# Two graph-attention layers on one core: attention units visited in pairs, three visits a step in place of six

## The chip, the cores and the metric

The kernel runs on one core of one Trainium2 chip. The metric is the device time of one execution in microseconds. Three runs of the kernel before gave 3366.99, 3367.01 and 3368.44 us; the median is 3367.01 us.

## What is computed

64 graphs of 256 nodes with 512 features go through two layers. Each layer normalises the rows, takes the positive part, runs attention over the graph's edges and adds the result to its input. The reference, cut to what matters:

```python
# layer 0: 4 heads of 64, adjacency as mask
h = jnp.maximum(_layernorm(x, axis=-1), 0.0)
q, k, v = h @ Wq, h @ Wk, h @ Wv                       # split in 4 heads
sim = jnp.einsum('bhid,bhjd->bhij', q, k) * scale
attn = softmax(where(adj, sim, -max))
x = x + einsum('bhij,bhjd->bhid', attn, v) @ Wo + bo
# layer 1: 8 heads of 64, another layernorm with gamma and beta, mask = adj | eye
h = jnp.maximum(_layernorm(x, axis=-1), 0.0)
...
x = x + (probs @ v) @ w_out.T + b_out
```

All is in f32.

## The kernel before

**Step and units.** A step works on two graphs (G = 2), so there are 32 steps. Two heads make a *unit* (`pr`): layer 0 has two units a step and layer 1 four, so six a step and 192 in all. The steps overlap: while step s runs its layer 1, step s+1 finishes layer 0 and step s+2 starts it.

**Products.** The projections (`project_qk` L769, `project_v1` L810) and the output products (`combine` L826) each run a two-by-two block product in seven block products instead of eight. That needs sums of blocks, which GpSimd (POOL) forms (`act_sums0`, `act_sums1`, L409 to L414). The seven results are put together by VectorE (DVE) and ScalarE (ACT) in `evacuate` and `accumulate`. Each product writes one of four PSUM banks, handed round by `mm_tile`. `project_v0` (L796) is plain.

**A unit of attention** goes through these pieces:

- `scores` (L877): eight matmuls on half the array each (64 rows, two at once), into four PSUM tiles `sc`, one for each graph g and head e. A tile is 128x512 f32. The pool of these tiles, `ps_sc`, has four buffers.
- `mask_scores` (L901): DVE adds the mask to one score tile and writes `p` in SBUF; four for a unit.
- `exponentials` (L906): ACT, four for a unit, in place on `p`.
- `key_halves` (L911): POOL adds the two halves over keys into `pd`, two for a unit.
- `weigh` (L920): sixteen matmuls on 32 columns each (four at once) into one tile of the same pool `sc`; ACT copies it to `oT` (L937).
- `key_sums` (L953): four matmuls of `pd` with ones, the softmax's denominators, into an `mm` bank.
- `invert` (L963, L964): DVE takes the reciprocals in two halves, and one more operation keeps the extremes. Eight small DMAs (L978), issued by SyncE (SP), spread the result over partitions into `invb`.
- `normalise` (L983): POOL multiplies `oT` by `invb`.

**A visit** joins the end of one unit with the start of another: weighing, sums and inversion of a unit `prev`, then scores and masks of a unit `cur`, whose exponentials and key halves follow.

**What sets the order.** On PE, DVE, ACT and POOL the order is written out by hand: `at(period, place, fn, ...)` collects events, which are sorted by `period * PERIOD + place` and issued in that order. A whole set of seven products has length 1 on this scale, and a step has 6.2. SP is not on the list. [...]

**Order of a step on PE before**, from place 0.0: a visit, then `project_qk` (s,1,0); at 1.0 a visit, `project_v1`; at 2.0 a visit, `project_qk` (s,1,1); at 3.0 a visit, `transpose_h` of s+2 and `combine` of layer 0 of s+1; at 3.64 a visit, `project_qk` (s+2,0,0); at 4.64 a visit, `project_v0`; at 5.2 `transpose_h` of s+1 and `combine` of layer 1 of s.

Of the kernel before, what the change touches and what calls it, by code (L numbers as in the profile page):

```python
# [315 lines left out]
def fast_path(  # L316
# [136 lines left out]
    def weight_loads():  # L453

        pair = act.tile([P, 2, 4, D], FP, name="wr", tag="oT1")
        blocks = [
            pair[:, 0], pair[:, 1],
            act.tile([P, 4, D], FP, name="wr", tag="v1"), io.tile([P, 4, D], FP, name="wr", tag="xt"),
        ]
        for n, wr in enumerate(blocks):  # L460
            src, r0 = (w_qkv, 4 * n) if n < 3 else (w_out, 0)
            nc.sync.dma_start(wr, src[r0 * P:(r0 + 4) * P].rearrange("(r p) i -> p r i", p=P))
        return blocks

    def weight_block(wr, n, c):
        pw = mm_tile([P, 4 * P])
        for r in range(4):
            nc.tensor.transpose(pw[:, r * P:(r + 1) * P], wr[:, r, c * P:(c + 1) * P], ident)
        for i in range(2):
            blk = A_OF[i, c // HC]  # L470
            dst = wqkv1[:, blk, c % HC, n, :] if n < 3 else wo1[:, blk, c % HC, :]
            copy = nc.vector.tensor_copy if i == 0 and (n or c == 0) else nc.scalar.copy
            copy(dst, pw[:, i * H1:(i + 1) * H1])  # L473
# [16 lines left out]
    def load_x(s):  # L490
        xt = io.tile([P, NT, D], FP, name="xt")
        nc.sync.dma_start(xt, x[s * G:(s + 1) * G].rearrange("g (t p) d -> p (g t) d", p=P))
        S[s]["xt"] = xt
# [259 lines left out]
    def project_qk(s, lyr, a, n):  # L753
# [3 lines left out]
        if n == 1:  # L757
            for i, pr in enumerate((a, a + half)):
                if (s, lyr, a) == (NSTEP - 1, 1, 0):
                    tile_qk = wqk0[:, 2 * i:2 * i + 2].rearrange("p n c k o -> p n (c k o)")  # L760
                else:
                    tile_qk = sm.tile([P, 2, T], FP, name="qk", bufs=2)
                st["qk", lyr, pr] = tile_qk
# [101 lines left out]

    units = [0]

    def scores(s, lyr, pr):
# [17 lines left out]
        elif last and pr == 3:  # L886
            p = [act.tile([P, G, NIC, N], FP, name="p", tag=tag) for tag in ("oT0", "v0")]
        else:
            p = [sm.tile([P, G, NIC, N], FP, name="p", bufs=4) for _ in range(2)]
        if last and pr in (1, 2):  # L890
            pd = (wo0[:, :4, 0, :], wv0)[pr - 1].rearrange("p a b -> p (a b)").rearrange("p (e g n) -> p e g n", e=2, g=G)
        else:
            pd = sm.tile([P, 2, G, N], FP, name="pd", bufs=1)
# [14 lines left out]
    def key_halves(s, lyr, pr, e):  # L908
        p, pd = S[s]["p", lyr, pr]
        eng = nc.vector if (s, lyr) == (NSTEP - 1, 1) and pr in (1, 3) else nc.gpsimd  # L910
        eng.tensor_tensor(pd[:, e], p[e][:, :, 0, :], p[e][:, :, 1, :], ALU.add)  # L911

    def weigh(s, lyr, pr, first):
# [11 lines left out]
        if lyr == 0:  # L925
            if first:
                st["oT0"] = act.tile([P, NB, HP0, N], FP, name="oT0")
        elif first:
            st["oT1"] = act.tile([P, NB, HP1, N], FP, name="oT1")
# [5 lines left out]
    def weigh_out(s, lyr, pr, first):  # L935
        po, dst = weigh(s, lyr, pr, first)
# [3 lines left out]
    def weigh_last(pr):  # L940

        po, dst = weigh(NSTEP - 1, 1, pr, pr == 0)
        nc.vector.tensor_tensor(dst, po, S[NSTEP - 1]["invb", 1, pr], ALU.mult)

    def key_sums(s, lyr, pr):

        st = S[s]
        _, pd = st["p", lyr, pr]
        sums = st["sums", lyr, pr] = mm_tile([P, N])
        for g in range(G):  # L950
            for e in range(2):
                r0 = 32 * (2 * g + e)
                nc.tensor.matmul(  # L953
                    sums[r0:r0 + 32, :], ones, pd[:, e, g, :], start=True, stop=True
                )

    def invert(s, lyr, pr):
        st = S[s]
        sums = st.pop(("sums", lyr, pr))
        last = (s, lyr) == (NSTEP - 1, 1)  # L960
        inv = sm.tile([P, N], FP, name="inv", tag="u" if last and pr == 3 else "inv", bufs=1)
        for i in range(2):
            nc.vector.reciprocal(inv[:, i * P:(i + 1) * P], sums[:, i * P:(i + 1) * P])  # L963
# [5 lines left out]
        if last and pr:  # L969
            invb = act.tile([P, G, N], FP, name="invb", tag=("n0", "ne", "ab")[pr - 1])  # L970
        else:
            invb = sm.tile([P, G, N], FP, name="invb", bufs=1)
        for g in range(G):
            for e in range(2):
                r0 = 32 * (2 * g + e)
                for d0 in range(e * DH, (e + 1) * DH, 32):
                    queue = nc.scalar if d0 % DH and last and pr in (1, 3) else nc.sync
                    queue.dma_start(invb[d0:d0 + 32, g, :], inv[r0:r0 + 32, :])  # L978
# [10 lines left out]
    PERIOD = 6.2  # L989
# [3 lines left out]
    def at(period, place, fn, *args):  # L993
        events.append((period * PERIOD + place, len(events), fn, args))
# [15 lines left out]
    def visit(period, w, prev, cur):  # L1010

        w -= 0.0003
        if 0 <= prev[0] < NSTEP:
            at(period, w, weigh_out, *prev)
            at(period, w, key_sums, *prev[:3])
            at(period, w, invert, *prev[:3])
            at(period, w + (0.63 if prev[1:3] == (1, 1) else 0.55), normalise, *prev[:3])
        if 0 <= cur[0] < NSTEP:
            at(period, w, scores, *cur)
            at(period, w, mask_scores, *cur, 0)  # L1020
            at(period, w + 0.05, exponentials, *cur, 0)
            at(period, w + 1 / 7, mask_scores, *cur, 1)
            at(period, w + 0.22, exponentials, *cur, 1)
            at(period, w + 0.23, key_halves, *cur, 0)
            at(period, w + 0.3, key_halves, *cur, 1)

    AT_C0, AT_Q0, AT_V0, AT_H1, AT_C1 = 3.0, 3.64, 4.64, 5.2, 5.201
    LAST_QK = 3.0
    for s in range(-1, NSTEP - 1):
        p, tail = s, s == NSTEP - 2  # L1030
        if s >= 0:
            visit(p, 0.0, (s + 1, 0, 0, True), (s + 1, 0, 1))
            visit(p, 1.0, (s + 1, 0, 1, False), (s, 1, 0))
        visit(p, 2.0, (s, 1, 0, True), (s, 1, 2))
        visit(p, 3.0, (s, 1, 2, False), (s, 1, 1))
        visit(p, LAST_QK + 4 / 7 if tail else AT_Q0, (s, 1, 1, False), (s, 1, 3))
        if s >= 0:
            visit(p, LAST_QK + 1 if tail else AT_V0, (s, 1, 3, False), (s + 1, 1, 0) if tail else (s + 2, 0, 0))

    none = (NSTEP,)  # L1040
    p = NSTEP - 2
    for w, i, pr in ((1, 5 / 7, 0), (1 + 3 / 7, 5 / 7, 2), (2, 5 / 7, 1), (2 + 3 / 7, 5 / 7, 3)):
        if pr:
            visit(p, LAST_QK + w, none, (NSTEP - 1, 1, pr))
        at(p, LAST_QK + w + i - 0.0005, key_sums, NSTEP - 1, 1, pr)
        at(p, LAST_QK + w + i, invert, NSTEP - 1, 1, pr)
# [4 lines left out]
    visit(-2, AT_V0, (-1, 0, 0, True), (0, 0, 0))  # L1051
    visit(-2, AT_H1, (0, 0, 0, True), (0, 0, 1))
    visit(-2, AT_H1 + 0.67, (0, 0, 1, False), (-1, 0, 0))
    visit(-1, 2.3, (-1, 0, 0, False), (1, 0, 0))
    for s in range(NSTEP):

        p = s - 2
        if s == 1:
            p -= 3.93 / PERIOD
        at(p - 1 if s != 1 else -2, 5.7 if s != 1 else 3.2, load_h, s)  # L1060
        at(p, (2.0, 2.4)[s] if s < 2 else 0.2, adjacency_cast, s)
        for t in range(NT):
# [3 lines left out]
            else:  # L1066
                at(p, 2.3 + 0.1 * t if s != 1 else 2.6 + 0.1 * t, scale_row, s, t)
        for g in range(G):
            at(p, (1.8, 2.7)[s] if s < 2 else 0.58 + 0.14 * g, neighbours, s, g)
        if s < 2:  # L1070
            at(p, (2.9, 2.72)[s], neighbours_rows, s)
            at(p, (AT_Q0 + 0.285, 3.59)[s], neighbours_turn, s)
        else:
            at(p, 0.75, neighbours_out, s)
            at(p, 1.9, neighbours_in, s)
        at(p, (AT_Q0 + 0.1425, 3.583)[s] if s < 2 else 2.2, adjacency_turn, s)
        at(p, (AT_Q0 + 0.3, 3.74)[s] if s < 2 else 2.75, mask0, s)
        at(p, (AT_Q0 + 0.31, 4.43)[s] if s < 2 else 5.7, mask1, s)
        if s == 0:
            at(p, AT_C0, first_transposes)  # L1080
# [3 lines left out]
        at(p, AT_C0 + 0.1, lambda s=s: act_sums0(S[s]["hT"]))  # L1084
        at(p, AT_C0 + (0.35 if s > 1 else 0.101 if s else 0.2), lambda s=s: act_sums1(S[s]["hT"]))
        order = SET if s else (1, 2, 6, 5, 7, 3, 4)
        at_set(p, AT_Q0 if s != 1 else 3.3, order, project_qk, s, 0, 0)
        for t in range(NT):
            at_dense(p, AT_V0 + 0.14 * t + (-0.0005 if s == 0 and t == 0 else 0) if s != 1 else (4.31, 5.02, 5.16, 5.31)[t], 0.14, project_v0, s, t)
        p = s - 1  # L1090
        if s == 0:
            p -= 2.23 / PERIOD
        at(p, 0.0 if s == 0 else 1.0 if s < NSTEP - 1 else 0.7, load_x, s)
        at(p, 1.55 if s == 0 else 1.8 if s < NSTEP - 1 else 1.25, first_bias, s)
        if 0 < s < NSTEP - 1:
            at(p, 1.75, lambda s=s: act_sums0(S[s]["oT0"]))
            at(p, 1.76, lambda s=s: act_sums1(S[s]["oT0"]))
        edge = 0 if s == 0 else 1 if s == NSTEP - 1 else 2
        for i, n in enumerate(SETC0 if 0 < s < NSTEP - 1 else NORM1):
            if edge == 0:  # L1100
                at_dense(p, 2.76 + 0.14 * i, 0.14, combine_rows, s, n)
            elif edge == 1:
                at_dense(p, 1.99905 + 0.00014 * i, 0.00113, combine_rows, s, n)
# [111 lines left out]
```

## Time and profile before

| What | Value |
|---|---|
| median of three runs | 3367.01 us |
| the profiled execution's own time | 3368.43 us |
| its span | 3366.6 us |
| granted TensorE clock | 0.999 |
| score matmuls, L877 with tiles `qk` | 3040 records, 380.3 us busy |
| weighing matmuls, L920 | 6144 records, 370.7 us busy |
| mask adds, L901 | 768, 478.6 us busy, 682 ns each |
| reciprocals, L963 | 384, 339.7 us busy, 926 ns each |
| key halves on POOL, L911 | 378, 472.5 us busy, 1271 ns each |
| inverses spread by DMA, L978 | 1528 issues on SP of 32 KB each, 1.9 us to landing |

One f32 matmul leaves two records. A record's duration is longer than the distance between two starts, since matmuls are pipelined, so lengths on PE are best taken from start to start. In the kernel's order of time a step repeats every 104.07 us from the second to the last but one (the first product of `project_v1` starts at 1045.27 us and again at 1149.34 us).

### The profile page before, as it was taken

To read this page: it belongs to the slowest core of one execution; us is meant where nothing else is said; L and a number is where in the kernel's file an instruction comes from. 1 tells how busy PE (TensorE), PEld (TensorE's weight loads), DVE (VectorE), ACT (ScalarE), POOL (GpSimd) and SP (SyncE) were. 2 spreads that over 40 slices of the span, in tenths; PEclk is the share of its full clock that TensorE was granted. 3 is DMA by queue.
4 is the path that set the end of the run, shared out by engine and by line. 5 is a ranking of instruction groups with operands and counts; after the bars stand their busy time and mean duration, and the time that the engine had idled before them with its cause. 6 is when DMAs were issued, how large, how long until landed. Compare 5 with 4: busy or idle time off the path is not lost.

```text
span 3366.6 us, 60168 instructions
## 1 busy us (share of the span) xinstructions
PE 3349.3 (99%) x22962; PEld 2688.2 (80%) x22962; DVE 1938.0 (58%) x3460; ACT 1230.5 (37%) x2218; POOL 2215.4 (66%) x2112
## 2 busy tenths in 40 slices
PE   8999999999999999999999999999999999999999
PEld 6788887888888888888888788887888878888877
DVE  6655556555565555555555655556555565565656
ACT  4333333333343334433344333443333333334331
POOL 6766775666766667666676566775667766667642
PEclk9999999999999999999999999999999999999999
DMA  3122111221112211112211121111111111211111
GB/s 130 46 59 57 54 32 47 58 59 53 32 50 56 58 54 34 48 57 56 59 42 46 46 58 57 54 34 46 59 58 53 32 49 56 59 53 34 48 38 46
DMA packets 168135, 174.10 MB, mean 52 GB/s; under 512 B 59672, under 2 KB 113056, under 8 KB 167840
## 3 DMA queue, kind: packets, MB, share of 16 engines
q1 hardware_dynamic: 167024, 169.52, 17.6%
q8 instruction: 184, 3.01, 0.5%
q14 instruction: 111, 0.91, 0.1%
q10 hardware_dynamic: 816, 0.66, 0.1%
HBM read 86.12 MB, written 33.62 MB: 36 GB/s over the span
## 4 chain that ended last, share of the span: by engine, by line
PE 98%; DMA 1%; SPq 0%; DVE 0%; ACT 0%; POOL 0%; issue 0%; POOLq 0%; DVEq 0%
PE mm L769 34%; PE mm L826 17%; PE mm L810 12%; PE sc L877 11%; PE sc L920 11%; PE mm L796 7%; PE mm L661 3%; PE mm L953 2%; PE mm L549 0%; DMA h<-in_x_dram 0%; PE mm L852 0%; SPq L978 0%; DMA wv<-in_L_gnn_Wv_dram 0%; DMA invb<-inv 0%; DVE bs L576 0%; POOL xt L498 0%
## 5 line engine op out<-in xcount | busy, mean ns | idle before, releaser
L911 POOL TENSOR_TENSOR pd<-p 128x512 f32<-128x512 f32 x378 | 472.5, 1271 | 508.9 <-ACT p L906 508.8
L769 PE MATMUL mm<-hT,wqkv 128*128 128x256 f32 x3584 | 798.0, 382 | 0.0
L769 PEld LDWEIGHTS mm<-hT,wqkv 128*128 128x128 f32 x3584 | 674.4, 190 | 108.5 <-issue 21.2
L906 ACT ACTIVATE p<-p 128x512 f32<-128x512 f32 x768 | 457.6, 631 | 465.6 <-DVE p L901 462.9
L826 PE MATMUL mm<-wo,oT 128*128 128x256 f32 x2632 | 585.7, 381 | 0.0
L963 DVE RECIPROCAL inv<-mm 128x128 f32<-128x128 f32 x384 | 339.7, 926 | 372.6 <-PE mm L953 341.3
L826 PEld LDWEIGHTS mm<-wo,oT 128*128 128x128 f32 x2632 | 491.0, 190 | 76.9 <-DVE xt L722 9.7
L937 ACT COPY oT<-sc 128x512 f32<-128x512 f32 x188 | 110.0, 585 | 1068.0 <-PE sc L920 1054.8
L901 DVE TENSOR_TENSOR p<-sc,n 128x512 f32<-128x512 f32 x768 | 478.6, 682 | 2.9 <-PE sc L877 1.5
L769 PE MATMUL mm<-hT,wqk 128*128 128x256 f32 x1792 | 398.9, 383 | 0.9 <-DVE qk L705 0.9
L810 PE MATMUL mm<-wqkv,hT 128*128 128x256 f32 x1792 | 395.5, 381 | 0.0
L983 POOL TENSOR_TENSOR oT<-oT,invb 128x512 f32<-128x512 f32 x188 | 239.4, 1274 | 227.5 <-DMA invb<-inv 221.1
L769 PEld LDWEIGHTS mm<-hT,wqk 128*128 128x128 f32 x1792 | 337.6, 191 | 57.9 <-issue 11.5
L810 PEld LDWEIGHTS mm<-wqkv,hT 128*128 128x128 f32 x1792 | 338.5, 190 | 54.7 <-issue 10.7
L877 PE MATMUL sc<-qk 64*128 64x256 f32 x3040 | 380.3, 389 | 0.0
L920 PE MATMUL sc<-p,v 128*32 128x256 f32 x6144 | 370.7, 382 | 0.0
L877 PEld LDWEIGHTS sc<-qk 64*128 64x128 f32 x3040 | 278.6, 187 | 103.1 <-issue 65.0
L733 POOL TENSOR_TENSOR xt<-xt,u 128x512 f32<-128x512 f32 x183 | 230.5, 1274 | 164.6 <-DVE xt L727 149.9
L920 PEld LDWEIGHTS sc<-p,v 128*32 128x32 f32 x6144 | 180.7, 110 | 161.3 <-issue 62.0
L722 DVE TENSOR_TENSOR xt<-mm,xt 128x512 f32<-128x512 f32 x124 | 85.4, 689 | 324.2 <-PE mm L826 324.1
L592 ACT ACTIVATE h<-h,mr,r 128x512 f32<-128x512 f32 x252 | 196.9, 807 | 126.5 <-POOL mr L588 118.0
L796 PE MATMUL mm<-wv,hT 128*128 128x256 f32 x1024 | 230.3, 383 | 0.3 <-ACT wqkv L473 0.3
(135 smaller groups left out, 3672.5 us busy)
## 6 DMA issues: line engine op xcount, KB each, us to landing
invb<-inv SPq DMA_DIRECT2D x1528, 32.0 KB, 1.9
xt<-in_x_dram SPq DMA_DIRECT2D x32, 1024.0 KB, 5.6
h<-in_x_dram SPq DMA_DIRECT2D x31, 1024.0 KB, 5.4
out_dram<-xt SPq DMA_DIRECT2D x31, 1024.0 KB, 4.5
ne<-row SPq DMA_DIRECT2D x30, 256.0 KB, 4.6
ad<-in_adj_dram SPq DMA_DIRECT2D x32, 128.0 KB, 11.1
wr<-in_L_gnn_w_qkv_dram SPq DMA_DIRECT2D x3, 1024.0 KB, 13.1
h<-in_x_dram SPq DMA_DIRECT2D x4, 256.0 KB, 3.6
```

The costliest lines, as they stand in the source:

```text
L733: (nc.vector if last else nc.gpsimd).tensor_tensor(r, r, u, ALU.add)
L769: nc.tensor.matmul(bank[:, k, :], w[:, wa, c, k, a * P:(a + 1) * P], st["hT"][:, ba, c, :], start=first and (k, c) == (0, 0), stop=(k, c) ...
L796: nc.tensor.matmul(bank, st["hT"][:, b0 + t // NIC * step, c % HC, i:i + P], wv0[:, c, :], start=(c == 0), stop=(c == NC - 1),)
L810: nc.tensor.matmul(bank[:, t, :], st["hT"][:, ba, c, t * P:(t + 1) * P], wqkv1[:, wa, c, 2, :], start=first and (t, c) == (0, 0), stop=(t, ...
L826: nc.tensor.matmul(bank[:, t, :], oT[:, ba, c, t * P:(t + 1) * P], w[:, wa, c, :], start=first and (t, c) == (0, 0), stop=(t, c) == (NIC - ...
L877: nc.tensor.matmul(sc[g][e][:, kc, :], qk[rows, 1, k0:k0 + P], qk[rows, 0, g * N:(g + 1) * N], start=True, stop=True,)
L901: nc.vector.tensor_tensor(p[e][:, g], sc[e], neg[:, :, g, :], ALU.add)
L906: nc.scalar.activation(p[e][:, g], p[e][:, g], AF.Exp, scale=SCALE)
L911: eng.tensor_tensor(pd[:, e], p[e][:, :, 0, :], p[e][:, :, 1, :], ALU.add)
L920: nc.tensor.matmul(po[r0:r0 + 32, g, :], st[f"v{lyr}"][:, g * NIC + kc, pr * P + r0:pr * P + r0 + 32], p[r0 // DH][:, g, kc, :], start=(kc ...
L963: nc.vector.reciprocal(inv[:, i * P:(i + 1) * P], sums[:, i * P:(i + 1) * P])
L983: nc.gpsimd.tensor_tensor(dst, dst, invb, ALU.mult)
```

## The change

Units are visited in pairs. `visit` takes a tuple of units on each side. It issues the key sums of both finished units into one `mm` bank (`key_sums` with `prs`), then both weighings, then the scores of both new units. The pool `ps_sc` keeps its four buffers. The second half of the second unit's reciprocal, with what follows it, stands behind the masks of the first new unit. A step has three such visits: at 2.0, at 4.64 and at 6.36.

Both layers' weighed values share one place: `place_values` makes one tile `oT` for either layer, and parts of it that the block sums use later hold the reciprocals and their spread copies until then. `pd` gets two buffers.

The order of a step becomes, on PE: `project_qk` (s,1,0) at 0.0, `combine` of layer 1 of s-1 at 1.0, a paired visit at 2.0 with `project_v1`, `project_qk` (s,1,1) at 3.0, `transpose_h` of s+2 and `combine` of layer 0 of s+1 at 4.0, a paired visit at 4.64 with `project_qk` (s+2,0,0), `project_v0` at 5.64, `transpose_h` of s+1 at 6.21, a paired visit at 6.36. The unit of the scale is as before; the step's number on it is 6.4. In the first step visits stay single, and in the last the pairs have no weighing of the last units before all four are weighed together (`weigh_last`). The second layer's weights are loaded one block after another, and some sums of weights move from DVE to POOL. In the last step key halves are all on POOL and the small DMAs all on SP.

```diff
     def visit(period, w, prev, cur):
         w -= 0.0003
-        if 0 <= prev[0] < NSTEP:
-            at(period, w, weigh_out, *prev)
-            at(period, w, key_sums, *prev[:3])
-            at(period, w, invert, *prev[:3])
-            at(period, w + (0.63 if prev[1:3] == (1, 1) else 0.55), normalise, *prev[:3])
-        if 0 <= cur[0] < NSTEP:
-            at(period, w, scores, *cur)
-            at(period, w, mask_scores, *cur, 0)
-            at(period, w + 0.05, exponentials, *cur, 0)
-            at(period, w + 1 / 7, mask_scores, *cur, 1)
-            at(period, w + 0.22, exponentials, *cur, 1)
-            at(period, w + 0.23, key_halves, *cur, 0)
-            at(period, w + 0.3, key_halves, *cur, 1)
+        s, lyr, prs = prev
+        last = (s, lyr) == (NSTEP - 1, 1)
+        if prs:
+            at(period, w, key_sums, s, lyr, prs)
+            if prs[0] == 0 and not last:
+                at(period, w, place_values, s, lyr)
+            for i, pr in enumerate(prs):
+                k = i if len(prs) > 1 else pr % 2
+                at(period, w + 0.1 * last, invert, s, lyr, pr, k, (0,) if i and not last else (0, 1))
+                if not last:
+                    at(period, w, weigh_out, s, lyr, pr)
+                    at(period, w + (0.55 if len(prs) == 1 else (0.3, 0.75)[i]), normalise, s, lyr, pr)
+        for i, pr in enumerate(cur[2]):
+            unit = (*cur[:2], pr)
+            one = len(cur[2]) == 1
+            at(period, w, scores, *unit)
+            at(period, w, mask_scores, *unit, 0)
+            at(period, w + 1 / 7 if one else w, mask_scores, *unit, 1)
+            if i == 0 and len(prs) > 1 and not last:
+                at(period, w, invert, s, lyr, prs[1], 1, (1,))
+            for g, place in enumerate((0.05, 0.22) if one else ((0.02, 0.03), (0.15, 0.3))[i]):
+                at(period, w + place, exponentials, *unit, g)
+            for e, place in enumerate((0.23, 0.3) if one else ((0.1, 0.11), (0.35, 0.36))[i]):
+                at(period, w + place, key_halves, *unit, e)
...
-    def key_sums(s, lyr, pr):
+    def key_sums(s, lyr, prs):
         st = S[s]
-        _, pd = st["p", lyr, pr]
-        sums = st["sums", lyr, pr] = mm_tile([P, N])
-        for g in range(G):
-            for e in range(2):
-                r0 = 32 * (2 * g + e)
-                nc.tensor.matmul(
-                    sums[r0:r0 + 32, :], ones, pd[:, e, g, :], start=True, stop=True
-                )
+        bank = mm_tile([P, 2, N])
+        for i, pr in enumerate(prs):
+            _, pd = st["p", lyr, pr]
+            st["sums", lyr, pr] = bank[:, i]
+            for g in range(G):
+                for e in range(2):
+                    r0 = 32 * (2 * g + e)
+                    nc.tensor.matmul(
+                        bank[r0:r0 + 32, i, :], ones, pd[:, e, g, :], start=True, stop=True,
+                        skip_group_check=True,
+                    )
...
+    def place_values(s, lyr):
+        st = S[s]
+        tile_o = act.tile([P, NB, HP1, N], FP, name="oT")
+        if lyr:
+            st["oT1"] = tile_o
+            st["invb"] = [tile_o[:, 3], tile_o[:, 4]]
+            st["inv"] = [tile_o[:, 6, i] for i in range(2)]
+        else:
+            flat = tile_o.rearrange("p b c n -> p (b c) n")
+            st["oT0"] = flat[:, :NB].rearrange("p (b c) n -> p b c n", c=HP0)
+            st["invb"] = [flat[:, 8:10], flat[:, 10:12]]
+            st["inv"] = [flat[:, 12 + i] for i in range(2)]
...
-        if last and pr in (1, 2):
-            pd = (wo0[:, :4, 0, :], wv0)[pr - 1].rearrange("p a b -> p (a b)").rearrange("p (e g n) -> p e g n", e=2, g=G)
-        else:
-            pd = sm.tile([P, 2, G, N], FP, name="pd", bufs=1)
+        pd = sm.tile([P, 2, G, N], FP, name="pd", bufs=2)
...
-    AT_C0, AT_Q0, AT_V0, AT_H1, AT_C1 = 3.0, 3.64, 4.64, 5.2, 5.201
-    LAST_QK = 3.0
...
+    AT_X, AT_C0, AT_Q0, AT_V0, AT_H1, AT_Z = 2.0, 4.0, 4.64, 5.64, 6.21, 6.36
+    LAST_QK = 4.0
+    none, L0, L1A, L1B = (NSTEP, 0, ()), (0, 1), (0, 2), (1, 3)
+    for s in range(NSTEP - 1):
+        visit(s, AT_X, (s + 1, 0, L0), (s, 1, L1A))
+        if s < NSTEP - 2:
+            visit(s, AT_Q0, (s, 1, L1A), (s, 1, L1B))
+            visit(s, AT_Z, (s, 1, L1B), (s + 2, 0, L0))
...
             at_set(p, 0.0, SET, project_qk, s, 1, 0)
-            at_set(p, 1.0, SET, project_v1, s)
-            at_set(p, 2.0, SET, project_qk, s, 1, 1)
+            at_set(p, 2.0, SET, project_v1, s)
+            at_set(p, 3.0, SET, project_qk, s, 1, 1)
+            p, place = (s + 1, 1.0) if s < NSTEP - 2 else (s, LAST_QK + 2)
...
+            at_set(p, place, SETC, combine, s, 1)
+            at(p, place + 1.05, store, s)
```

## The prediction

> **What bounds the kernel now.** I read the page's busy shares first, then the chain that ended last, then what TensorE (PE) waited for, then PE's timeline over one step. The first two leave no doubt about the engine:
>
> ```profile
> PE 3349.3 (99%) x22962; PEld 2688.2 (80%) x22962; DVE 1938.0 (58%) x3460; ACT 1230.5 (37%) x2218; POOL 2215.4 (66%) x2112
> ...
> PE 98%; DMA 1%; SPq 0%; DVE 0%; ACT 0%; POOL 0%; issue 0%; POOLq 0%; DVEq 0%
> ```
>
> The list of PE's waits holds only 10 us in all, nearly all in the first 100 us; its longest entry is the start:
>
> ```profile
> PE mm L682 <- ACT h L618: 7.1, 3, 6.6
> ```
>
> So the time is the length of PE's instruction stream, and an edit counts by the PE slots it removes or the PE waits it makes. One visit of before, all engines (start, length, engine, line):
>
> ```profile
> 1041.05 1.93 PE L920 MATMUL sc<-p,v 128*32 128x256 f32 x32
> 1042.80 0.61 PE L953 MATMUL mm<-pd,ones 128*32 128x256 f32 x8
> 1043.05 0.58 ACT L937 COPY oT<-sc 128x512 f32<-128x512 f32 x1 [6.43 <-PE sc L920]
> 1043.34 2.00 PE L877 MATMUL sc<-qk 64*128 64x256 f32 x16
> ...
> 1043.48 1.77 DVE L963 RECIPROCAL inv<-mm 128x128 f32<-128x128 f32 x2 [1.64 <-DMA xt<-in_x_dram]
> ...
> 1045.27 12.36 PE L810 MATMUL mm<-wqkv,hT 128*128 128x256 f32 x56
> 1045.28 0.43 DVE L964 CUSTOM_DVE_ANT_0 mm<-mm,inv 128x256 f32<-128x256 f32 x1
> ...
> 1045.63 2.48 DVE L901 TENSOR_TENSOR p<-sc,n 128x512 f32<-128x512 f32 x4
> ```
>
> Look at two things: PE goes from weighing to sums to scores to products without a hole, and the four mask adds (DVE L901) that empty the score banks take 2.48 us but run beside products, when nobody waits for them.
>
> The price of a change of array shape comes from two stretches of products of one kind in the last step, each between the same neighbours:
>
> ```profile
> 3273.12 7.17 PE L769 MATMUL mm<-hT,wqkv 128*128 128x256 f32 x32
> 3280.23 1.94 PE L920 MATMUL sc<-p,v 128*32 128x256 f32 x32
> ...
> 3284.45 5.45 PE L769 MATMUL mm<-hT,wqkv 128*128 128x256 f32 x24
> 3289.83 1.94 PE L920 MATMUL sc<-p,v 128*32 128x256 f32 x32
> ```
>
> Start to start, 32 records take 7.11 us and 24 take 5.38: 0.216 us a record (a slot), and 5.38 - 24 x 0.216 = 0.20 us for the stretch's two ends.
>
> **What the Trainium skill says.** TensorEngine Tiling (Array Packing), Key Properties: changing the tiling mode drains TensorE. The trace agrees: the 0.20 us above. The same page, PSUM Bottleneck: tiling speeds up TensorE and not the evacuation of PSUM, which may become the bottleneck. In before it doesn't show, since each visit makes four score tiles for four buffers. PSUM — Partial Sum Buffer, Specifications: 8 banks of 2 KiB a partition. A score tile of 512 f32 fills one; the sc pool's four and the four mm banks are all there are. TensorE: Matmul & The Clock Gate, Part 3: matmuls keep program order, so a score matmul waiting for its bank holds every later product. The only such wait of before is in the last step:
>
> ```profile
> 3252.25 2.69 PE L877 MATMUL sc<-qk 64*128 64x256 f32 x16
> ...
> 3253.19 0.57 ACT L937 COPY oT<-sc 128x512 f32<-128x512 f32 x1
> 3253.81 0.73 PEld L877 LDWEIGHTS sc<-qk 64*128 64x128 f32 x6 [0.40 <-ACT oT L937]
> ...
> 3254.87 1.35 PE L769 MATMUL mm<-hT,wqkv 128*128 128x256 f32 x5
> ```
>
> PE resumes 0.05 us after the copy's end (3253.19 + 0.57 = 3253.76), and from there to the products it takes 1.06 us for four slots: 4 x 0.216 + 0.10 for the restart + 0.10 for the switch.
>
> **Part 1, pairing: switches saved.** In one visit, start to start: weighing 1.75 us for 8 slots (32 records, four at once), sums 0.54 for 2, scores 1.93 for 8 (16, two at once). Over 0.216 a slot this leaves 0.02 + 0.11 + 0.20, and the following products' two ends 0.20: 0.53 us a visit. A pair does two units' sums, two weighings, two units' scores, with one set of switches: the slots stay, 0.53 us goes. Matmuls and their sizes are otherwise unchanged.
>
> **Part 2, pairing: the score banks.** The changed PE order is sums, weighing, weighing, 8 score matmuls of the first unit, 8 of the second, back to back, and the sc pool still has four buffers. The weighings take banks a and b, the first unit's g0 scores c and d, g1 a and b, the second unit's g0 c and d again, g1 a and b. The second unit therefore waits for the first unit's mask adds. Let S be the start of the scores. g0's fourth slot starts at S + 0.32 + 2 x 0.216 = 0.75 and lasts 0.38 (the row's median record): 1.13. DVE follows PE after 0.07 (sums end 1042.80 + 0.61 = 1043.41, reciprocal 1043.48): first mask at S + 1.20. The four end at S + 1.20 + 2.48 = 3.68. After that release only half the second unit's g1 is left, four slots: 0.05 + 1.06, so products start at S + 4.79. Without the wait it would be 16 x 0.216 + 0.20 = 3.66. The stall is 1.13 us.
>
> Is DVE free at S + 1.20? From the start K of the visit, the last product's evacuation (0.69 us) ends near K + 0.8; three reciprocals at 0.89, one L964 (0.43) and its readout (0.14) end near K + 4.1; S is at K + 20 x 0.216 + 0.1 = 4.4. Yes, by 1.5 us. Is the second weighing's bank free for g1? Its ACT copy starts about S + 0.1 and takes 0.58; g1 begins at S + 0.97. Yes, by 0.2 us. The other half of the second reciprocal and L964 stand behind these masks and delay only the second unit's adds, done by about S + 7.6; the first DVE evacuation after the visit is due near S + 8.6.
>
> **Part 3, what moves behind.** SP issues eight invb DMAs in 4.94 us:
>
> ```profile
> 1132.89 4.94 SPq L978 DMA_DIRECT2D invb<-inv  x8
> ```
>
> A pair has sixteen, the second eight after its late reciprocal, landed near K + 16.5, also past the x load or h load now between them. POOL then normalises (1.27), behind four key halves (1.27 each, done near K + 16), and forms sums of oT. Their user is combine, whose first summed block is due about K + 23 in the tightest case (layer 1, now after a whole product set), against K + 19 to 20. The copies and exponentials of a pair (8 x 0.63 on ACT) end near K + 13, beside the first three products. Key sums come at least 30 us after their scores. The tightest of all: layer-1 normalisation is 1 us ahead of transpose_h at 6.21. I cost these at nothing; if a cover of 1 us fails once a step, it is 31 us. The single oT place adds DVE and ACT waits on readers that finished just before: nothing, up to 0.3 us. Below nothing no part can go, as PE had no hole to give back.
>
> **Part 4, the ends.** First and last steps: the last step of before had four lone key sums and three lone scores, some 2 us of switches, now merged. At the start PE's holes sum to about 5 us; weight loads are serialised. I take -2, from -6 to +6.
>
> **Sum.** Each pair with scores: -0.53 + 1.13 = +0.60 us. Of 192 units two at the start stay single: 95 pairs. 95 x 0.60 = 57, less 2: +55 us, of which a full step, 104.07 us now (V product 1045.27 to 1149.34), takes +1.8. On the profiled execution (span 3366.6, its time 3368.43) this gives 3423.4; the median 3367.01 lies 1.4 lower, so 3422.
>
> **Rivals.**
> - Faster: the banks come free in time and only switches go: 95 x -0.53 - 2 = -52, 3315 us. It decides if the fourth mask ends before S + 3.08 in place of S + 3.68, which asks adds of 0.45 us apart where the trace has 0.60. Against it: DVE's duration and the unchanged four buffers. 10%, for any reading that the profile can't show.
> - The stall as worked and a second wait on top, once a step: transpose_h behind ScalarE's scaled rows, or combine behind POOL's sums, by 1 us: 55 + 31, 3453; with DVE late by 1 us before all three mask groups too, 3546. For it: two covers under 2 us or so. 18%.
> - Stall and saving cancel: net within 0.07 us a pair, 3367. It needs a stall of half the size. 4%.
> - My likeliest, 68%: 3422, own range 3405 to 3438.
>
> **How the numbers follow.** The range 3398 to 3458 holds the likeliest and the nearer half of the second rival. A measurement here tells 0.2% (6.7 us) from no change: faster 0.10, same 0.04, slower 0.86.
>
> **What would show it.** In the profile after: step 105.9 us; score groups of a pair about 4.8 us where twice 1.93 was before; PE waiting at the scores for DVE p L901 about 95 x 1.1 = 105 us (part of it may read as busy, since ends are modelled); one set of shape switches fewer for each pair. Wrong if scores of a pair take 3.7 us, or if PE's new waits stand at products, transposes or combine.

## The result, and the profile after

The changed kernel takes 3424.21 us (median of four runs, 3423.92 to 3425.59), beside 3367.52 us for the kernel before on the same chip: a ratio of 1.0169, 95% interval 1.0151 to 1.0186. The profiled execution's span is 3422.6 us, 55.9 us above the 3366.6 us of before. In the kernel's own rhythm a step is 105.94 us from one set of adjacency transposes to the next, where it was 104.07.

The page of the kernel before has these two groups for its scores (busy us, mean ns of one, then idle time before them and what ended most of it):

```profile
L877 PE MATMUL sc<-qk 64*128 64x256 f32 x3040 | 380.3, 389 | 0.0
L877 PEld LDWEIGHTS sc<-qk 64*128 64x128 f32 x3040 | 278.6, 187 | 103.1 <-issue 65.0
```

The page of the changed kernel, busy time (engine, us, share of the span, instructions), the chain that ended last, and the score groups:

```profile
PE 3403.6 (99%) x22962; PEld 2741.9 (80%) x22962; DVE 1960.1 (57%) x3445; ACT 1253.6 (37%) x2221; POOL 2239.5 (65%) x2124
...
PE 85%; POOL 13%; issue 1%; DVE 1%; DMA 1%; SPq 0%; ACT 0%; POOLq 0%
...
L875 PE MATMUL sc<-qk 64*128 64x256 f32 x3072 | 462.9, 402 | 2.3
L875 PEld LDWEIGHTS sc<-qk 64*128 64x128 f32 x3072 | 314.7, 186 | 151.3 <-DVE p L899 75.9
```

PE executes as many matmuls as before and still reads 99% busy. Its score matmuls went from 380 us busy, which left out 32 records listed under another tile's name, to 463. The list of PE's waits stays almost empty, since a matmul's end is modelled and overlaps the next start: at the wait for the fourth mask, two starts are 0.28 us apart, where a record lasts 0.38. The row of the weight loads shows who is waited for: 151 us idle before the score weights, half of it ended by DVE's mask add `p` L899. Before, that row had 103 us idle, and no mask add among its first releasers. A page that says 99% busy can hide a wait of 1.1 us in each visit.

The chain that ended last names POOL with 13%, where the kernel before had 0%. In one visit of a step a score matmul of the second unit resumes 0.04 us after the end of a sum on POOL (L413), and the chain follows POOL back from there. It isn't the matmul that ends the pair's scores. In experiment 1 below POOL is as busy as here (2241 us), its share of the chain is 0%, and the step is 3.39 us shorter, so POOL's share is no cause of the loss.

The timeline of one paired visit of the changed kernel (start, length, engine, line; other lines left out; PEld is a weight load):

```profile
1056.08 3.64 PE L931 MATMUL sc<-p,v 128*32 128x256 f32 x64
1056.39 1.77 DVE L983 RECIPROCAL oT<-mm 128x128 f32<-128x128 f32 x2 [0.39 <-PE mm L961]
...
1058.72 0.96 DVE L983 RECIPROCAL oT<-mm 128x128 f32<-128x128 f32 x1
1059.65 4.83 PE L875 MATMUL sc<-qk 64*128 64x256 f32 x32
1059.79 0.59 ACT L943 COPY oT<-sc 128x512 f32<-128x512 f32 x1 [1.10 <-PE sc L931]
1060.82 2.48 DVE L899 TENSOR_TENSOR p<-sc,n 128x512 f32<-128x512 f32 x4 [1.14 <-PE sc L875]
...
1063.35 0.73 PEld L875 LDWEIGHTS sc<-qk 64*128 64x128 f32 x6 [0.30 <-DVE p L899]
...
1064.41 3.94 PE L807 MATMUL mm<-wqkv,hT 128*128 128x256 f32 x17
```

Read it from the scores' start S = 1059.65. The first mask add starts at S + 1.17, the four end at S + 3.65, and the products begin at S + 4.76. The wait comes in pieces, as the adds free one bank after another; the last weight loads start at 1063.35, 0.05 us after the fourth add's end at 1063.30. The scores of before took 1.93 us for one unit, 3.86 for two; 32 records here take 4.76.

### The profile page after: what moved, and what is told of

Same layout as the page of the kernel before. It is cut to its first block, busy times and chain, and to the rows that moved or that the text cites. A ratio compares the mean times of both kernels' runs of the same rounds, so it can differ in the third digit from the quotient of the medians.

```text
span 3422.6 us, 59964 instructions
## 1 busy us (share of the span) xinstructions
PE 3403.6 (99%) x22962; PEld 2741.9 (80%) x22962; DVE 1960.1 (57%) x3445; ACT 1253.6 (37%) x2221; POOL 2239.5 (65%) x2124
## 4 chain that ended last, share of the span: by engine, by line
PE 85%; POOL 13%; issue 1%; DVE 1%; DMA 1%; SPq 0%; ACT 0%; POOLq 0%
PE mm L766 33%; PE mm L823 17%; PE sc L875 12%; PE mm L807 12%; PE sc L931 7%; POOL xt L639 4%; POOL qk L776 2%; PE mm L961 2%; PE mm L662 2%; POOL hT L412 1%; POOL hT L409 1%; POOL hT L413 1%; POOL n L569 1%; POOL r L587 1%; POOL n L572 1%
## 5 line engine op out<-in xcount | busy, mean ns | idle before, releaser
L766 PE MATMUL mm<-hT,wqkv 128*128 128x256 f32 x3584 | 787.4, 380 | 1.0 <-ACT wqkv L471 1.0
L899 DVE TENSOR_TENSOR p<-sc,n 128x512 f32<-128x512 f32 x766 | 475.0, 682 | 110.5 <-PE sc L875 109.1
L983 DVE RECIPROCAL oT<-mm 128x128 f32<-128x128 f32 x376 | 345.1, 939 | 290.0 <-PE mm L961 286.3
L904 ACT ACTIVATE p<-p 128x512 f32<-128x512 f32 x766 | 443.6, 627 | 174.9 <-DVE p L899 174.5
L875 PE MATMUL sc<-qk 64*128 64x256 f32 x3072 | 462.9, 402 | 2.3
L875 PEld LDWEIGHTS sc<-qk 64*128 64x128 f32 x3072 | 314.7, 186 | 151.3 <-DVE p L899 75.9
L931 PE MATMUL sc<-p,v 128*32 128x256 f32 x6128 | 349.9, 379 | 0.4 <-issue 0.4
L931 PEld LDWEIGHTS sc<-p,v 128*32 128x32 f32 x6128 | 199.8, 110 | 132.2 <-issue 1.2
L1000 POOL TENSOR_TENSOR oT<-oT 128x512 f32<-128x512 f32 x188 | 239.3, 1273 | 60.3 <-DMA oT<-oT 54.0
L793 PEld LDWEIGHTS mm<-wv,hT 128*128 128x128 f32 x1024 | 194.3, 190 | 27.1 <-issue 0.6
L409 POOL TENSOR_TENSOR hT<-hT 128x512 f32<-128x512 f32 x64 | 81.7, 1277 | 185.7 <-ACT hT L666 174.6
```

What stands on the lines that cost most here:

```text
L766: nc.tensor.matmul(bank[:, k, :], w[:, wa, c, k, a * P:(a + 1) * P], st["hT"][:, ba, c, :], start=first and (k, c) == (0, 0), stop=(k, c) ...
L793: nc.tensor.matmul(bank, st["hT"][:, b0 + t // NIC * step, c % HC, i:i + P], wv0[:, c, :], start=(c == 0), stop=(c == NC - 1),)
L875: nc.tensor.matmul(sc[g][e][:, kc, :], qk[rows, 1, k0:k0 + P], qk[rows, 0, g * N:(g + 1) * N], start=True, stop=True,)
L899: nc.vector.tensor_tensor(p[e][:, g], sc[e], neg[:, :, g, :], ALU.add)
L904: nc.scalar.activation(p[e][:, g], p[e][:, g], AF.Exp, scale=SCALE)
L931: nc.tensor.matmul(po[r0:r0 + 32, g, :], st[f"v{lyr}"][:, g * NIC + kc, pr * P + r0:pr * P + r0 + 32], p[r0 // DH][:, g, kc, :], start=(kc ...
```

## Experiments

All are edits of the changed kernel. The first two and the last give part of the score tiles another pool; the others move one piece of the visit. The number beside each is its median and its ratio to the kernel before, which took 3368.2 to 3368.4 us beside them; experiment 5 ran once and has no ratio.

**1. The second unit's g0 tiles in the mm banks.**

```diff
-    def scores(s, lyr, pr):
+    def scores(s, lyr, pr, second=False):
...
-        sc = [[ps_sc.tile([P, NIC, N], FP, name="sc") for e in range(2)] for g in range(G)]
+        sc = [
+            [mm_tile([P, NIC, N]) if second and g == 0 else ps_sc.tile([P, NIC, N], FP, name="sc") for e in range(2)]
+            for g in range(G)
+        ]
...
-            at(period, w, scores, *unit)
+            at(period, w, scores, *unit, i == 1)
```

> Paired visits as in the changed kernel, but the second unit's g0 score tiles come from the mm banks, so its g1 tiles take the two sc buffers that the first two mask adds free (by S + 2.5 us, when PE is at S + 2.75). Theory (the wait for score banks, 1.13 us a pair, hides a saving of 0.53 us in array switches): no wait is left, scores of a pair 3.66 us in place of 4.8, 95 x -1.13 = -107 us: 3317 us, 50 below the kernel before. Rival 1 (the pair is slower for another reason than banks, DVE's queue or ACT's copies): scores stay at 4.8 us, 3424. Rival 2 (the wait moves to the products, whose mm banks are now taken): scores 3.7 but the first product sets grow, total 3340 to 3424.

Measured: 3326.74 us, ratio 0.9878 (0.9861 to 0.9894). The timeline of the same kind of visit:

```profile
1029.45 2.00 PE L878 MATMUL sc<-qk 64*128 64x256 f32 x16
...
1030.62 2.49 DVE L902 TENSOR_TENSOR p<-sc,n 128x512 f32<-128x512 f32 x4 [1.14 <-PE sc L878]
1031.28 1.03 PE L878 MATMUL mm<-qk 64*128 64x256 f32 x8
...
1032.15 1.03 PE L878 MATMUL sc<-qk 64*128 64x256 f32 x8
...
1033.11 7.17 PE L807 MATMUL mm<-wqkv,hT 128*128 128x256 f32 x32
```

The masks start as late as in the changed kernel (S + 1.17) and take as long. Only the banks differ, and the scores of a pair fall from 4.76 to 3.66 us (1029.45 to 1033.11). So the wait for the banks is shown, and so is what it had covered: a step takes 102.55 us, 1.52 below the kernel before, 0.51 a pair. The total missed its 3317 by 10 us: 2 in the steps, and most of the rest in the last step. There PE stood still in the output products:

```profile
3265.08 1.99 PE L823 MATMUL mm<-wo,oT 128*128 128x256 f32 x8
3272.10 13.54 PE L823 MATMUL mm<-wo,oT 128*128 128x256 f32 x48 [5.03 <-POOL pd L911]
```

From the end of the first product's last record to 3272.10 PE waits 5.03 us; the 48 records after it take 13.5 us where 48 x 0.216 is 10.4. The releaser named is POOL, but DVE's line ends at the same moment (next fence), and experiment 6 decides between them.

```profile
3271.50 0.43 DVE L989 CUSTOM_DVE_ANT_0 mm<-mm,bo_b 128x256 f32<-128x256 f32 x1
```

**2. The second unit's g1 tiles in the mm banks instead.** The edit is the first one with `g == 1`.

> As the run before, but the second unit's g1 tiles come from the mm banks; its g0 still takes the sc buffers freed by the first two mask adds. Theory: the last needed add ends at S + 1.20 + 1.29 = 2.49, PE resumes at 2.54 and has 8 slots left (half of g0, all of g1) of 0.216 plus 0.20: products at S + 4.47, a wait of 0.81 us in place of 1.13; 95 x -0.32 = -30 us: 3394 us. Rival (any two more banks do, the number counts and not which tile waits): 3317 as in the run before. Rival (not the banks): 3424.

Measured: 3402.04 us, ratio 1.0101 (1.0084 to 1.0117). The step is 104.95 us, 0.99 below the changed kernel's, 0.33 a pair where 0.32 was worked out. Start to start, the scores of a pair take 4.43 or 4.50 us, depending on the visit. The same two extra banks give a gain of 22 us at the one place and 97 us at the other, so their number is not what counts: what counts is which mask add the tile at hand has to wait for. The total is 8 us over the expectation; a wait of 4.2 us in the last step, like that of the first experiment, is in it.

**3. Sums, weighing, scores, weighing, scores.**

```diff
-                at(period, w + 0.1 * last, invert, s, lyr, pr, k, (0,) if i and not last else (0, 1))
+                if not (i and not last):
+                    at(period, w + 0.1 * last, invert, s, lyr, pr, k)
                 if not last:
-                    at(period, w, weigh_out, s, lyr, pr)
+                    if not (i and len(cur[2]) > 1):
+                        at(period, w, weigh_out, s, lyr, pr)
...
+            if i and len(prs) > 1 and not last:
+                at(period, w, weigh_out, s, lyr, prs[1])
             at(period, w, scores, *unit)
...
-                at(period, w, invert, s, lyr, prs[1], 1, (1,))
+                at(period, w, invert, s, lyr, prs[1], 1)
```

> The pair's PE order becomes sums, weighing, scores, weighing, scores, with the second unit's inversion after the first unit's masks: the second weighing fills the time in which the masks free the banks. Theory: no wait on banks, but one more change between column and row tiles, 0.11 + 0.20 us; against the kernel before 95 x (-0.53 + 0.31) - 2 = -23 us: 3344 us. Rival (changes of array shape cost less than read, and the pair's loss is something else): no better than the changed kernel, 3424. If a wait stays for the second weighing's bank or ACT's copy, each 0.1 us a pair adds 10 us.

Measured: 3354.17 us, ratio 0.9962 (0.9948 to 0.9976). It is faster than both kernels without any more banks: the second weighing runs while DVE empties the score tiles.

```profile
1005.43 1.91 PE L931 MATMUL sc<-p,v 128*32 128x256 f32 x32
...
1007.27 2.00 PE L875 MATMUL sc<-qk 64*128 64x256 f32 x16
...
1009.25 1.93 PE L931 MATMUL sc<-p,v 128*32 128x256 f32 x32
...
1011.12 2.00 PE L875 MATMUL sc<-qk 64*128 64x256 f32 x16
...
1013.04 7.82 PE L766 MATMUL mm<-hT,wqkv 128*128 128x256 f32 x35
```

The step takes 103.62 us, 1.07 above the first experiment's, 0.36 a pair: the price of one more change from rows to columns and back, for which 0.31 was worked out. That leaves 0.15 us a pair against the kernel before, not 0.22, which is 6.5 us of the 10 by which the expectation missed; one wait of 2.0 us for ACT's copy, outside the steady steps, is in the rest.

**4. The whole inversion ahead of the masks.**

```diff
-                at(period, w + 0.1 * last, invert, s, lyr, pr, k, (0,) if i and not last else (0, 1))
+                at(period, w + 0.1 * last, invert, s, lyr, pr, k)
...
-            if i == 0 and len(prs) > 1 and not last:
-                at(period, w, invert, s, lyr, prs[1], 1, (1,))
```

> The second unit's whole inversion stands ahead of the first unit's masks, 1.45 us more on DVE before them. Theory: DVE has 1.5 us to spare there, so nothing moves: 3424 us, up to 3434 if the reserve is 0.1 us short. Rival (DVE's queue ahead of the masks sets the wait): 95 x 1.45 = 138 us more, 3560.

Measured: 3430.66 us, ratio 1.0186 (1.0169 to 1.0203); a step of 106.08 us, 0.05 a pair more than the changed kernel. The reserve is real but smaller than worked out. DVE sat idle 1.14 us before the masks in the changed kernel's fence above. Here it has none left:

```profile
1028.39 4.94 PE L875 MATMUL sc<-qk 64*128 64x256 f32 x32
...
1029.67 0.14 DVE L986 DVE_READ_ACCUMULATOR2_ANT extremes<- 128x1 f32 x1
1029.67 4.87 DVE L899 TENSOR_TENSOR p<-sc,n 128x512 f32<-128x512 f32 x8
```

The masks follow the inversion without a gap and start at S + 1.28. In the same visit of the step the changed kernel has them at S + 1.24 (1025.99 to 1027.23 us), so they are 0.04 us late, and the pair is longer by as much. DVE's own queue was not what made the pair slow, but with no idle time left before the masks a further operation there would come on top.

**5. The half inversion between the first unit's g0 and g1 masks.** The edit moves the late `invert`, with its condition, above the second `mask_scores`.

> The second unit's half reciprocal and what follows it (0.89 + 0.43 + 0.14 = 1.46 us on DVE) stand between the first unit's g0 and g1 masks. Theory: the fourth mask ends 1.46 us later and PE waits for it: scores of a pair about 6.2 us, 93 pairs x 1.4 = +130 us: 3554 us. Rival (the fourth mask is not what PE waits for, the first two decide): 3424.

Measured: 3576.16 us in its one run; its span is 3574.3 us. One visit, with the half inversion between the adds:

```profile
1066.45 3.71 PE L875 MATMUL sc<-qk 64*128 64x256 f32 x24
...
1068.90 0.95 DVE L983 RECIPROCAL oT<-mm 128x128 f32<-128x128 f32 x1
...
1070.23 3.68 DVE L899 TENSOR_TENSOR p<-sc,n 128x512 f32<-128x512 f32 x6
...
1070.97 1.73 PE L875 MATMUL sc<-qk 64*128 64x256 f32 x8 [0.81 <-DVE p L899]
```

In most visits the fourth add ends at S + 4.99 where the changed kernel has S + 3.65, and the scores of a pair take 6.10 us, start to start, where it has 4.76. Both are 1.34 more. The rival, that the first two adds decide, asks for no change. The steady step is 109.95 us, so this mechanism accounts for 4.01 x 31 = 124 of the 152 us that the span grew. Another 21 us are in eight steps that are longer than 109.95, told in the last section; without them the total would be near the 3554 expected.

**6. The first experiment, with all tiles from the sc pool in the one visit whose finished units are the last step's own.** The argument becomes `i == 1 and not last`.

> As the run with the second unit's g0 tiles in mm banks, except in the one visit of the last step where the finished units are the last step's own (there all score tiles are from the sc pool). In the first run PE stood 5.0 us in that visit's output products, and 13 records after it ran at 0.427 us in place of 0.216, which is 2.7 us more. Theory: the mm bank of the key sums, released only by the late inversion, was the bank that these products wanted; with two more mm banks free it isn't wanted so early. 3326.7 - 5.0 - 2.7 + 1.1 (this one pair waits for its sc buffers again) = 3320 us. Rival (the products wait for POOL's key halves, which the trace names): 3327 us.

Measured: 3320.14 us, ratio 0.9859 (0.9843 to 0.9876), the fastest of all. The last step's output products now run without a hole:

```profile
3260.86 4.83 PE L878 MATMUL sc<-qk 64*128 64x256 f32 x32
3265.62 12.35 PE L823 MATMUL mm<-wo,oT 128*128 128x256 f32 x56
...
3271.11 1.27 POOL L911 TENSOR_TENSOR pd<-p 128x512 f32<-128x512 f32 x1
```

The key halves on POOL end at 3272.38 us, later in the visit than in the first experiment, and the products run past them. So the products didn't wait for POOL, though the trace named it, but for an mm bank, of which two more are free here. That it was the key sums' own, released by L989, fits the moment (3271.50 + 0.43 = 3271.93, PE at 3272.10). It also follows from the kernel's text: `mm_tile` hands out the four banks in turn, so in the first experiment the key sums, the two g0 tiles and the first product take one each, and the second product gets the bank of the sums again. Here only the fifth product does, at 3272.6 us, when the same operation of DVE has ended (3271.4).

## Why the prediction was right

Forecast 3422 us, measured 3424.2, by the mechanism forecast. By its steps:

- **The bound.** That the time is PE's instruction stream held in every run: steps of 102.55 to 109.95 us give the totals, with the ends of the program adding or taking a few us, and the eight longer steps of experiment 5 apart.
- **Part 1, switches.** Priced at 0.53 us a pair from two product stretches of unlike length. With the bank wait taken away, the saving is (104.07 - 102.55) / 3 = 0.51. Experiment 3 adds one change back and pays 0.36 for it, where the same prices gave 0.31. The total was right, but not all its parts. Over a step the sums save 0.61 us (0.33 priced), the scores 0.61 (0.60), products and transposes 0.50 (0.60), and the weighings cost 0.19 more (0.06 less priced). Sums and weighings have changed places, so the errors of these two cancel in part.
- **Part 2, banks.** Priced at 1.13 us a pair. Taking the wait away gives (105.94 - 102.55) / 3 = 1.13. Its parts are in the timeline: first mask at S + 1.17 (1.20 forecast), fourth end at S + 3.65 (3.68), products at S + 4.76 (4.79). Experiments 2 and 5 shorten and lengthen the time to the deciding mask by a known amount, and the pair follows within 0.06 us. The net is +0.62 us a pair; +0.60 was forecast. One reading beside it falls short: that before has four score tiles for four buffers leaves out the weighing's tile in the same pool. In the visit of before that the prediction shows, the four adds end at 1048.11 us, and the next weighing starts at 1057.55, so the products between them covered the adds.
- **DVE's reserve.** Forecast 1.5 us, measured 1.14. The reciprocals start later after the sums than counted: in the fence of the visit DVE is idle 0.39 us first and then takes 1.77 for two. It cost nothing, and experiment 4, which uses it up, shows how large it was.
- **Part 3, what moves behind.** Taken at nothing. PE's wait list shows no such wait in the steady steps, but it leaves out the waits for banks too, so it can't settle this. Lengths from start to start can. In a step the changed kernel's scores take 14.35 us and those of experiment 1 take 10.96, and all else on PE takes 91.59 us in both. Products and transposes together are 78.2 us, where before had 78.7. So no wait was added behind the visits.
- **Part 4, the ends.** -2 us forecast. The 95 pairs at 0.62 make 59 us, the span grew by 55.9: -3. This is a remainder that no run takes apart.

The rival that ended faster has its mark wrong. With the fourth mask's end at S + 3.08, and 1.11 us from there to the products as in Part 2, they would start at S + 4.19. That is 0.53 us after the 3.66 without a wait, so stall and saving would only cancel, which is the third rival. For 3315 us the fourth mask must end by 3.66 - 1.11 = S + 2.55, with adds 0.34 us apart. Nothing made the masks faster (their end was S + 3.65), so neither rival came; but experiment 6 reaches 3320 by sparing PE the need of the fourth mask.

## What to carry to other kernels

Grouping instructions of one array shape saves the changes of shape, here about 0.5 us for each visit less, but it also groups their outputs: count how many PSUM tiles the group writes, and when the engine that empties them will have emptied the one that the group needs again. If the answer is later than TensorE gets there, put other work of TensorE in between, or take the early tiles of the second group from banks that stand idle at that moment, so that the wait falls where it is already over. A buffer's place in the rotation can be worth more than one more buffer: the same two banks gave 22 or 97 us.

## What the runs showed that was not expected

A long wait on TensorE can cost more than itself. After the 5.03 us in the first experiment's last step, 12 records started 0.427 us apart in place of 0.216. The 4.2 us of the second experiment were followed by 11 such records, the 2.0 us of the third by none. In experiment 5 PE waits some 1.2 us, start to start, for the fourth mask in most visits, and twelve times in the run a stretch of records goes at 0.427; one of them, in PE's timeline:

```profile
2172.17 2.67 PE L875 MATMUL sc<-qk 64*128 64x256 f32 x8 [0.81 <-DVE p L899]
2174.77 14.71 PE L766 MATMUL mm<-hT,wqkv 128*128 128x256 f32 x56
```

The eight records take 2.60 us to the products, where most visits of that run need 1.66 (1070.97 to 1072.63 us), and the 56 products 14.5 in place of 12.3. The windows view gives the granted clock, as a share of full speed: 0.91 on average from 2160 to 2200 us, and 0.50 from 2173 to 2179 us.

In the trace's record of the clock the twelve stretches at half speed last 3.41 us (nine of them) or 6.83 us, and their starts lie whole multiples of 3.413 us apart (the first two 771.41 us, which is 226 times that). So they follow a fixed beat, while most visits with the same wait go at full speed. That a visit is hit when its waits fall in a certain way on this beat is likely but not shown. In the changed kernel, whose single waits are shorter, that record shows full speed from 16 us on until the last 4 us.

The Trainium skill, TensorE: Matmul & The Clock Gate, Part 1, puts TensorE at half its rate after an idle window of about 3.4 us. The rate agrees, and so do the waits of 5.03, 4.2 and 2.0 us. In experiment 5 no single pause is that long, so this statement alone doesn't account for it; how much pausing within which time brings it on, these runs don't settle.
